# From cross attention to the experts of a decoder layer: three shared groups in source order, with the routing's last steps and the experts' tables between their products

## The chip, the cores and the metric

The kernel runs on one core of a Trainium2 chip. A core has a matrix engine (TensorE, in the profile PE for the products and PEld for its weight loads), three engines for elementwise work (VectorE or DVE, ScalarE or ACT, GpSimd or POOL), and queues that issue transfers: SP for plain loads and stores, ACT for a few, POOL for indirect gathers and scatters. The metric is the device time of one execution in microseconds (us), taken as the median of several runs.

## The reference

A pre-norm decoder layer in float32, for 32 blocks of 128 tokens of 512 features, 4096 tokens in all. Three parts are added to `x` in turn, each on a layer norm of it:

```
x = x + attention(layernorm(x))          # differential self attention, 16 heads, per block
x = x + cross(layernorm(x), ctx)         # cross attention with rotary positions, 8 heads
x = x + ffn(layernorm(x))                # experts and a shared part
```

The last part is what the change touches:

```
scores = sigmoid(x @ gate_w)                       # 32 experts in 4 groups
# the 2 best groups by their best score; of their experts the 6 best
weights = scores of the 6, divided by their sum
expert_out = sum over the 6 of weight * (silu(x @ w_gate[e]) * (x @ w_up[e])) @ w_down[e]
shared = (silu(x @ sw_gate) * (x @ sw_up)) @ sw_down    # 704 wide, every token
return expert_out + shared
```

## The kernel before

The kernel has four stages, which follow each other on TensorE: self attention, cross attention, the experts, and the shared part for those blocks that have not had it earlier.

Cross attention (`CrossAttention`) is software-pipelined by hand. It counts steps, 16 to a block: each step does a piece of one block's scores (`maxima`, `exponentials`, `weigh`), and two lists of due times, `sooner` and `later`, hang other work on the step numbers. `plan` fills them. For block `b`, whose own steps begin at `16 * b`, the outputs leave 16 steps on: `divide` and `turn_out` (a transpose on TensorE each), `leave` (a product, and the store of x2 to `sum_d`), `hand_over` (the normalized h and its transpose are stored to DRAM as `h3_d` and `h3T_d`), `router` (a small product), and then the routing. `run` stops at the last step that has scores. What the last blocks still lack is done by `rest(count)`, which runs `count` more steps of the two lists alone.

The routing (`Routing`) picks for each token six experts. `groups`, `choose` and `take` work on DVE and POOL; `count` puts two small products on TensorE (L934, L935), to know how many tokens came to each expert before; `slots_of` and `enter` write, by an indirect transfer on POOL, each token's number and weight into a table in DRAM, sorted by expert (`table_d`, L951). After the last block `tiles` works out on DVE, in a row of some forty small instructions, which expert each tile of 128 table entries belongs to (`eid`, `fresh`, `rows`).

The shared part (`Shared.group`) works on four blocks at a time. For each of five chunks of 128 of the 704 columns it makes a gate and an up product (L1120, four instructions each of 128x512 outputs, eight records in the profile), a Silu on ACT (L1125) and a multiplication on DVE (L1126, into `s_gu`); the last 64 columns of gate and up share their products (L1134, L1141, L1142). Then, for each of two pairs of blocks, come the products with `sw_down` (L1152, and L1158 for the last chunk), the addition to x2 (`s_x2`, shown as `s_x`, L1162) and the store (L1164). Its inputs are loaded by `load` (`s_hT`, L1103) and at the head of each pair (L1148).

The experts (`Experts`) first gather the table by tiles (L1209), add its two halves (L1216), spread the entries (L1223) and transpose both on TensorE (L1218, L1228); from this come each tile's weights, the rows of DRAM to read (`run_of`, L1251) and to add to. `begin` issues the first tokens' gathers (`tokens`, L1304) and the first four sets of weights (L1278 and on, by SP, which reads the expert's number from `eid`). `run` goes through 208 tiles: `turn_in` (a transpose on DVE, L1316), `gate_up` (L1329), `turn_out` (L1355), `down` (L1365), and a scatter that adds to `sum_d` (L1370).

What orders the work: a scheduler places the instructions on each engine by their priorities and readiness. Inside `tc.manual_schedule(engines=...)` the named engines keep the order of the source. Before the change this holds for `CrossAttention.run` and `Experts.run` (TensorE, DVE, ACT, POOL; SP never), not for the shared groups between them. Each engine runs its own instructions in order.

Tiles come from pools. `cm.banks()` gives one of four PSUM buffers. The pool `s_p` of the shared part is opened when cross attention's pool of exponentials (`xp`) is closed, and lies on its memory; a tile there waits for the last reader of what it covers.

Between cross attention and the experts there are two shared groups (`EARLY = 2`). In the first, `between` is called after each chunk and at the end, and takes from `todo` the routing's last steps:

```
todo = [lambda: cross.rest(16)] * 6 + [
    lambda: routing.tiles(eid, fresh, rows, used, usual),
    lambda: nc.sync.dma_start(out=sum_d[T : T + P, :], in_=rest),
]
```

After it the `Experts` object is built, which includes the tables, then `experts.begin(0, usual)` and the second group. The other six groups come after the experts, with `final=True`, and store to the output.

Of the kernel before, what the change touches and what calls it, by code (L numbers as in the profile page):

```python
# [10 lines left out]
F32 = mybir.dt.float32  # L11
# [446 lines left out]
class CrossAttention:  # L458
# [264 lines left out]
    def plan(self, load_shared):  # L723
# [30 lines left out]
        later.put(20, load_shared)  # L754
        for b in range(self.B):
            sooner.put(2 * S * b - 11, self.measure, b)
# [330 lines left out]
class Shared:  # L1087
# [6 lines left out]
    def __init__(self, cm, pool, w, h3T_d, sum_d, out):  # L1094
        self.cm, self.pool, self.w, self.h3T_d, self.sum_d, self.out = cm, pool, w, h3T_d, sum_d, out
        self.NB = h3T_d.shape[0]
        self.hTs = {}

    def load(self, g):
        G = self.G  # L1100
        if g * G < self.NB and g not in self.hTs:
            self.hTs[g] = self.pool.tile([P, G, EC, P], F32, name="s_hT", bufs=2)
            self.cm.nc.sync.dma_start(  # L1103
                out=self.hTs[g], in_=self.h3T_d[ts(g, G)].rearrange("b p c t -> p b c t")
            )

    def group(self, g, final, between=lambda: None):
# [4 lines left out]
        self.load(g)  # L1112
        self.load(g + 1)
        hT = self.hTs.pop(g)
        gu = pool.tile([P, n + 1, G, P], F32, name="s_gu")
        for m in range(n):
            pgu = cm.banks().rearrange("p two (i t) -> p two i t", i=G)
            for i, part in enumerate((w.gate, w.up)):
                for c in range(EC):
# [3 lines left out]
                    )  # L1123
            act = pool.tile([P, G, P], F32, name="s_act", bufs=2)
# [19 lines left out]
        for pair in range(G // 2):  # L1144
            b = g * G + 2 * pair
            rows = self.sum_d[ts(b // 2, 2 * P), :].rearrange("(b p) e -> p b e", p=P)
            x2 = pool.tile([P, 2, E], F32, name="s_x2", bufs=2)
            nc.sync.dma_start(out=x2, in_=rows)  # L1148
            py = cm.banks()
            for i in range(2):  # L1150
                for m in range(n):
# [3 lines left out]
                    )  # L1155
            for i in range(2):
# [6 lines left out]
            to = self.out[b : b + 2].rearrange("b p e -> p b e") if final else rows  # L1163
            nc.sync.dma_start(out=to, in_=x2)  # L1164
        between()


class Experts:
# [14 lines left out]
    def __init__(  # L1183
# [14 lines left out]
        self.T = T  # L1198

        NT = rows.shape[1]  # L1200
        entry = cm.banks().rearrange("p o (j t) -> p o j t", j=EC)
        parts = cm.banks().rearrange("p o (t j x) -> p (o t) j x", t=2, j=2)
        for j in range(NT):
            got = [
                self.p2.tile([P, E], F32, name="e_y")[:, 0 : 2 * P].rearrange("p (s o) -> p s o", o=2)
                for i in range(len(table_ds))
            ]
            for t, table_d in zip(got, table_ds):
                nc.gpsimd.indirect_dma_start(  # L1209
                    out=t.rearrange("p s o -> p (s o)"),  # L1210
                    out_offset=None,
                    in_=table_d.rearrange("(n s) o -> n (s o)", s=P),
                    in_offset=bass.IndirectOffsetOnAxis(ap=rows[:, j : j + 1], axis=0),
                    bounds_check=table_d.shape[0] // P - 1,
                )
            nc.vector.tensor_tensor(got[0], got[0], got[1], ALU.add)  # L1216
            for o in range(2):
                nc.tensor.transpose(entry[:, o, j, :], got[0][:, :, o], cm.ident)  # L1218

            runs = self.p2.tile([P, self.Q, self.Q, 32], F32, name="e_xr", bufs=3)  # L1220
            slots = got[0][:, :, 0].rearrange("p (b t a) -> p t a b", b=self.Q, t=self.Q)
            for t in range(self.Q):
                nc.vector.tensor_copy(  # L1223
                    runs[:, t].rearrange("p q (a b) -> p q a b", b=self.Q),
                    slots[:, t].unsqueeze(1).broadcast_to([P, self.Q, 32 // self.Q, self.Q]),
                )
            for t in range(self.Q):
                nc.tensor.transpose(  # L1228
                    parts[:, t, j, :], runs[:, t].rearrange("p q i -> p (q i)"), cm.ident
                )  # L1230
        entry = entry.rearrange("p o j t -> p o (j t)")[:, :, 0:n_tiles]
        self.weight = cp.tile([P, n_tiles], F32, name="e_weight")
        nc.vector.tensor_copy(self.weight, entry[:, 1, :])

        row_i = cp.tile([P, 2], I32, name="e_row_i")
        nc.gpsimd.iota(row_i, pattern=[[0, 2]], base=T + 1, channel_multiplier=1)
        nc.vector.tensor_scalar(row_i[:, 1:2], row_i[:, 1:2], -T - 1, None, ALU.add)
        nc.vector.tensor_scalar(row_i[:, 1:2], row_i[:, 1:2], 5, None, ALU.logical_shift_right)
        row = cp.tile([P, 2], F32, name="e_row")
        nc.vector.tensor_copy(row, row_i)  # L1240
        none = cp.tile([P, n_tiles], F32, name="e_none")
        nc.vector.tensor_scalar(none, entry[:, 0, :], 0.0, row[:, 0:1], ALU.is_equal, ALU.mult)
        self.into = cp.tile([P, n_tiles], I32, name="e_into")
        nc.vector.scalar_tensor_tensor(self.into, entry[:, 0, :], -1.0, none, ALU.add, ALU.add)

        self.run_of = cp.tile([P, self.Q, NT * P], I32, name="e_run_of")
        nc.vector.tensor_scalar(
# [131 lines left out]
    def begin(self, first, end):  # L1379

        self.first, self.end, self.last = first, end, None
        for i in range(first, first + 3):
            self.tokens(i)
# [27 lines left out]
def decoder_kernel(  # L1411
# [32 lines left out]
    with tc.tile_pool(name="x_w", bufs=1, side="right") as x_w:  # L1444
# [40 lines left out]
        def between():  # L1485


            if todo:
                todo.pop(0)()
# [81 lines left out]
```

## Time and profile before

| what | value |
|---|---|
| median of 3 runs | 4184.48 us |
| lowest, highest | 4179.18, 4187.29 us |
| the profiled execution's own time | 4186.66 us |
| its span in the profile | 4184.9 us |
| its mean granted TensorE clock | 0.991 |
| TensorE, VectorE, ScalarE, GpSimd busy | 97%, 50%, 31%, 54% of the span |

The profile is of one execution. Its times are counted from the span's start. A line as L1120 is a line of the kernel before. In a timeline, a row gives the start, the length, the engine, the line, the instruction with what it writes and reads, how many follow each other, and in brackets the idle time before it and what ended that. Names are cut of their numbers, so that `s_x2` and `x1` read `s_x` and `x`. The granted clock is the share of full speed that TensorE was given.

Cross attention's last product ends at 2142.07, the experts' first begins at 2296.82, and the first final group's first product begins at 3833.28.

### The profile page before, as it was taken

Reading aid. Unit: us, or ns where it says so; the run is one execution under the profiler, and the core shown is the slowest. Engines: PE = TensorE matmul, PEld = TensorE weight load, DVE = VectorE, ACT = ScalarE, POOL = GpSimd, SP = SyncE. Lnnn points to the kernel's source line nnn. Section 1 sums busy time; section 2 is a strip of 40 time slices with the busy share of each in tenths; the row PEclk is TensorE's granted clock in tenths of the full one; section 3 lists DMA queues with packets and bytes.
Section 4 is the critical chain, followed back from the end, with each engine's and each line's share of the span. In section 5 each row is a group of like instructions: output and inputs, shape, how many; then the busy total and the mean of one; then the engine's idle time right before and its main releaser. Section 6 shows DMA issues by size and latency. Waiting matters only on the chain. (4 is left out here: it accounts for less than half of the span.)

```text
span 4184.9 us, 60374 instructions
## 1 busy us (share of the span) xinstructions
PE 4079.9 (97%) x21044; PEld 2154.4 (51%) x21044; DVE 2093.0 (50%) x3394; ACT 1296.3 (31%) x1855; POOL 2247.7 (54%) x2388
## 2 busy tenths in 40 slices
PE   7999999989999999999989999999999999999999
PEld 5666666653343444443434555555555555554444
DVE  4556555567788888888841333333333333332111
ACT  2333333334565555555630111111111111111000
POOL 3444444343455555555542777777777777773000
PEclk9999999999999999999999999999999999999999
DMA  3000000012111111111114677776776776775110
GB/s 103 26 29 29 29 31 29 16 36 82 41 44 46 44 44 41 44 44 44 36 61 145 164 168 171 165 186 159 169 168 164 168 182 154 185 164 130 60 61 30
DMA packets 282791, 386.33 MB, mean 92 GB/s; under 512 B 147792, under 2 KB 175056, under 8 KB 282448
## 3 DMA queue, kind: packets, MB, share of 16 engines
q0 software_dynamic: 62912, 109.85, 14.6%
q1 hardware_dynamic: 77680, 186.52, 13.6%
q10 hardware_dynamic: 141888, 86.01, 7.4%
q8 instruction: 170, 2.79, 0.3%
q14 instruction: 141, 1.16, 0.1%
HBM read 616.47 MB, written 142.02 MB: 181 GB/s over the span
## 5 line engine op out<-in xcount | busy, mean ns | idle before, releaser
L1304 POOL DMA_INDIRECT e_xr<-h_d,e_run_of x832 | 849.5, 1021 | 296.3 <-issue 246.2
L619 DVE TENSOR_REDUCE nm<-ps 128x2 f32<-128x1024 f32 x512 | 623.7, 1225 | 200.0 <-PE ps L615 131.9
L642 ACT ACTIVATE xp<-ps 128x1024 f32<-128x1024 f32 x512 | 517.1, 1024 | 422.3 <-PE ps L638 421.9
L1334 DVE TENSOR_TENSOR e_gu<-e_act,ps 128x352 f32<-128x352 f32 x208 | 108.6, 522 | 947.8 <-ACT e_act L1333 947.8
L1365 PE MATMUL ps<-wd,e_guT 128*128 128x512 f32 (+1 forms) x1248 | 570.2, 592 | 2.4 <-issue 2.3
L615 PE MATMUL ps<-xk,xq 32*128 32x512 f32 x2048 | 561.4, 635 | 1.6 <-POOL x_ln_down L66 1.1
L638 PE MATMUL ps<-xqn,xk 32*128 32x512 f32 x2048 | 548.8, 639 | 0.6 <-DVE xqn L627 0.6
L1329 PE MATMUL ps<-wg,e_xT 128*128 128x352 f32 x1664 | 529.0, 460 | 4.0 <-DMA wg<-in_L_ffn_w_gate_dram 4.0
L1329 PE MATMUL ps<-wu,e_xT 128*128 128x352 f32 x1664 | 527.2, 460 | 1.6 <-DMA wu<-in_L_ffn_w_up_dram 1.6
L1329 PEld LDWEIGHTS ps<-wg,e_xT 128*128 128x128 f32 x1664 | 315.4, 190 | 239.0 <-issue 105.9
L1329 PEld LDWEIGHTS ps<-wu,e_xT 128*128 128x128 f32 x1664 | 316.1, 190 | 179.7 <-DMA wu<-in_L_ffn_w_up_dram 4.3
L1370 POOL DMA_INDIRECT sum_d<-e_y,e_into x208 | 338.4, 1627 | 118.0 <-issue 70.3
L1333 ACT ACTIVATE e_act<-ps 128x352 f32<-128x352 f32 x208 | 96.4, 463 | 902.6 <-PE ps L1329 797.2
L1365 PEld LDWEIGHTS ps<-wd,e_guT 128*128 128x128 f32 (+1 forms) x1248 | 237.0, 190 | 247.4 <-issue 205.4
L1369 ACT ACTIVATE e_y<-ps,e_weight 128x512 f32<-128x512 f32 x208 | 142.9, 687 | 411.7 <-PE ps L1365 398.0
L615 PEld LDWEIGHTS ps<-xk,xq 32*128 32x128 f32 x2048 | 157.9, 183 | 212.1 <-ACT xp L642 100.7
L951 POOL DMA_INDIRECT table_d<-entry,at x192 | 196.6, 1024 | 109.9 <-DMA table_d<-entry,at 55.7
L1355 DVE STREAM_TRANSPOSE e_guT<-e_gr 96x384 f32<-96x384 f32 (+1 forms) x416 | 230.5, 554 | 47.7 <-DMA e_gr<-e_gu_d 40.4
L653 PE MATMUL ps<-xp,v 128*32 128x512 f32 x2048 | 248.1, 601 | 1.6 <-ACT xp L642 1.2
L1316 DVE STREAM_TRANSPOSE e_xT<-e_xr 128x512 f32<-128x512 f32 x208 | 226.9, 1091 | 6.5 <-DMA e_xr<-h_d,e_run_of 6.5
L229 POOL TENSOR_SCALAR k<-kz,a_keep,a_extra 128x256 f32<-128x256 f32 x128 | 83.4, 660 | 252.3 <-ACT kz L228 246.3
L228 ACT ACTIVATE kz<-ps,a_keep 128x256 f32<-128x256 f32 x128 | 53.7, 470 | 410.9 <-PE ps L222 410.9
(267 smaller groups left out, 5316.8 us busy)
## 6 DMA issues: line engine op xcount, KB each, us to landing
wg<-in_L_ffn_w_gate_dram SPq DMA_DIRECT2D x208, 704.0 KB
wu<-in_L_ffn_w_up_dram SPq DMA_DIRECT2D x208, 704.0 KB
wd<-in_L_ffn_w_down_dram SPq DMA_DIRECT2D x208, 576.0 KB
e_gu_d<-e_gu ACTq DMA_DIRECT2D x208, 192.0 KB
e_gr<-e_gu_d ACTq DMA_DIRECT2D x208, 192.0 KB
wd<-in_L_ffn_w_down_dram SPq DMA_DIRECT2D x208, 128.0 KB
e_xr<-h_d,e_run_of POOLq DMA_INDIRECT x832
xin<-in_x_dram SPq DMA_DIRECT2D x32, 256.0 KB
```

The costliest lines, as they stand in the source:

```text
L615: self.nc.tensor.matmul(sc[:, i, :], q[rows, ts(c, P)], k[rows, :], start=True, stop=True)
L619: self.nc.vector.tensor_reduce(at[:, self.ROW[side], 2 * pair : 2 * pair + 2], sc, AX.X, ALU.max, negate=True)
L638: self.nc.tensor.matmul(sc[:, i, :], k[rows, ts(c, P)], q[rows, :], start=True, stop=True)
L642: self.nc.scalar.activation(e, sc, AF.Exp)
L653: self.nc.tensor.matmul(po[b, side][ts(j, 32), :], self.v2[b % 2][:, c, 2 * j + side, :], es[j // 2][:, j % 2, :], start=c == 0, stop=c == ...
L951: self.nc.gpsimd.indirect_dma_start(out=self.table_ds[k % 2][:, :], out_offset=bass.IndirectOffsetOnAxis(ap=self.at[b][:, k : k + 1], axis=0),
L1304: self.cm.nc.gpsimd.indirect_dma_start(out=xr[:, t, :], out_offset=None, in_=self.h3_d.rearrange("t (q f) -> (t q) f", q=self.Q), in_offse ...
L1316: self.cm.nc.vector.transpose(xT.rearrange("p c (t i) -> p c t i", t=self.Q), self.xr.pop(i).rearrange("p t (j c) -> p c t j", c=EC),)
L1329: nc.tensor.matmul(pgu[:, half, 0:M], t[:, c, :], w[:, c, :], start=c == 0, stop=c == EC - 1)
L1355: self.cm.nc.vector.transpose(t[rows, 0:n, :].rearrange("p c (t i) -> p c t i", t=self.Q), g[rows, :, 0 : 32 * n].rearrange("p t (j c) -> ...
L1365: nc.tensor.matmul(py, t[:n, c, :], self.wd[s][:n, c, :], start=c == 0, stop=c == len(M_CHUNKS) - 1)
L1370: nc.gpsimd.indirect_dma_start(out=self.sum_d[:, :], out_offset=bass.IndirectOffsetOnAxis(ap=self.into[:, i : i + 1], axis=0), in_=y[:, :] ...
```

## The change

The third shared group moves from the end of the kernel to the passage between cross attention and the experts (`EARLY = 3`), so that five groups stay at the end. All three are now under `manual_schedule`, for TensorE, DVE, ACT and POOL.

`between` is called more often in a group: in the middle of each chunk too (after the gate products), and after each block's products within a pair; that is 15 times in a group. The routing's steps come in portions of two (`rest(2)`, 31 times) and spread over the first two groups; what is left of `todo` after them (one portion, `tiles` and one store) follows the second group.

`Experts.__init__` is cut up: `fetch` issues the gathers of the tables, `arrange` adds and spreads them on DVE, `turn_tables` transposes them on TensorE, `places` makes `run_of` and the rest, `first_tokens` gathers the first three tiles' tokens. `experts.begin` (the weights) and `fetch` stand ahead of the third group, the others are called between its products: both `arrange` after the fourth and fifth half chunks, `turn_tables` after the seventh, `places` after the eighth, `first_tokens` after the ninth. Half of the gathered tables are in buffers of `e_xT` instead of `e_y`.

The tiles `s_hT` come from a pool of their own, opened before cross attention's last pools, and the first of them is loaded from `plan`, at step `2 * S * (B - 2)`. The rows of x2 are loaded for a whole group at its head (`load_rows`), and for the third group ahead of `experts.begin`.

```diff
-    def plan(self, load_shared):
+    def plan(self, load_shared, load_tokens):
...
         later.put(20, load_shared)
+        later.put(2 * S * (self.B - 2), load_tokens)
...
     def load(self, g):
         G = self.G
         if g * G < self.NB and g not in self.hTs:
-            self.hTs[g] = self.pool.tile([P, G, EC, P], F32, name="s_hT", bufs=2)
+            self.hTs[g] = self.h_pool.tile([P, G, EC, P], F32, name="s_hT")
...
+    def load_rows(self, g):
+        if g not in self.x2s:
+            self.x2s[g] = []
+            for pair in range(self.G // 2):
+                x2 = self.pool.tile([P, 2, E], F32, name="s_x2", bufs=2)
+                self.cm.nc.sync.dma_start(out=x2, in_=self.rows_of(g, pair))
+                self.x2s[g].append(x2)
...
         self.load(g)
+        self.load_rows(g)
         self.load(g + 1)
...
                         pgu[:, i], part[:, c, ts(m, P)], hT[:, :, c, :],
                         start=c == 0, stop=c == EC - 1,
                     )
+                if i == 0:
+                    between()
...
                         py[:, i, :], gu[:, m, 2 * pair + i, :], w.down[:, m, :],
                         start=m == 0, stop=False,
                     )
+                between()
...
             nc.sync.dma_start(out=to, in_=x2)
-        between()
...
     def begin(self, first, end):
         self.first, self.end, self.last = first, end, None
-        for i in range(first, first + 3):
-            self.tokens(i)
         for i in range(first, first + SETS):
             self.weights_in(i)
             self.weights_out(i)
+
+    def first_tokens(self):
+        for i in range(self.first, self.first + 3):
+            self.tokens(i)
...
-        todo = [lambda: cross.rest(16)] * 6 + [
+        todo = [lambda: cross.rest(2)] * 31 + [
             lambda: routing.tiles(eid, fresh, rows, used, usual),
             lambda: nc.sync.dma_start(out=sum_d[T : T + P, :], in_=rest),
         ]
...
-        EARLY = 2
-        shared.group(0, False, between)
-        while todo:
-            between()
+        EARLY = 3
+        with tc.manual_schedule(engines=in_order):
+            for g in range(EARLY - 1):
+                shared.group(g, False, between)
+            while todo:
+                between()
     e_ctx = ctx.enter_context(ExitStack())
-    experts = Experts(
-        cm, e_ctx, table_ds, h3_d, sum_d, w_gate, w_up, w_down, eid, fresh, rows, n_tiles
-    )
-    experts.begin(0, usual)
-    for g in range(1, EARLY):
-        shared.group(g, False)
+    with tc.manual_schedule(engines=in_order):
+        experts = Experts(
+            cm, e_ctx, table_ds, h3_d, sum_d, w_gate, w_up, w_down, eid, fresh, rows, n_tiles
+        )
+        shared.load_rows(EARLY - 1)
+        experts.begin(0, usual)
+        experts.fetch()
+        nothing = lambda: None
+        todo += [nothing] * 3 + [
+            lambda: experts.arrange(0),
+            lambda: experts.arrange(1),
+            nothing,
+            experts.turn_tables,
+            experts.places,
+            experts.first_tokens,
+        ]
+        shared.group(EARLY - 1, False, between)
+        while todo:
+            between()
     experts.run()
```

`turn_tables` and `places` in the changed kernel, whose lines stood in `Experts.__init__`:

```
    def turn_tables(self):
        nc, cm = self.cm.nc, self.cm
        self.entry_ps = cm.banks().rearrange("p o (j t) -> p o j t", j=EC)
        self.parts_ps = cm.banks().rearrange("p o (t j x) -> p (o t) j x", t=2, j=2)
        for j in range(self.NT):
            got, runs = self.got.pop(j), self.spread.pop(j)
            for o in range(2):
                nc.tensor.transpose(self.entry_ps[:, o, j, :], got[0][:, :, o], cm.ident)
            for t in range(self.Q):
                nc.tensor.transpose(
                    self.parts_ps[:, t, j, :], runs[:, t].rearrange("p q i -> p (q i)"), cm.ident
                )

    def places(self):
        # e_weight, e_row_i, e_row; then run_of (two instructions over 128x1024), none, into
        ...
```

In the built order of the changed kernel, DVE has the two `turn_in` transposes of `Experts.run` directly ahead of the two multiplications of the third group's last chunk (those that stood at L1142).

## The prediction

> **What bounds the kernel now.** I read the page first (busy time, the slices), then the busy time by stretch, then TensorE's waits between cross attention and the experts, then the timelines of all engines there, last the chain that ended last.
>
> ```profile
> PE 4079.9 (97%) x21044; PEld 2154.4 (51%) x21044; DVE 2093.0 (50%) x3394; ACT 1296.3 (31%) x1855; POOL 2247.7 (54%) x2388
> PE   7999999989999999999989999999999999999999
> ```
>
> TensorE is busy 97% of the span and no other engine passes 54%. The change removes no product, so all it can win is time in which TensorE stands idle or runs slowly. Stretch by stretch (length, PE, PEld, DVE, ACT, POOL, granted clock, DMA share, GB/s):
>
> ```profile
> 2142.00:2297.00 155.00, 134.31 (x353) 63.77 (x352) 34.38 (x104) 17.40 (x26) 54.88 (x74) 0.92 0.41 126
> 2297.00:2354.00 57.00, 57.00 (x177) 33.52 (x178) 20.57 (x31) 7.83 (x14) 38.20 (x34) 1.00 0.59 142
> 3892.00:3950.00 58.00, 58.00 (x149) 26.39 (x146) 6.72 (x9) 3.74 (x7) 0.00 (x0) 1.00 0.16 55
> ```
>
> The experts and the final shared groups run without a gap at full clock. The passage between cross attention's last product (2142.07) and the experts' first (2296.82) lacks 21 us of busy time and has a granted clock of 0.92. TensorE's waits there (total, times, longest):
>
> ```profile
> PE ps L934 <- DVE taken L927: 6.1, 2, 3.3
> PE ps L1152 <- DVE s_gu L1126: 5.3, 1, 5.3
> PE ps L1120 <- DMA s_hT<-h3T_d: 4.6, 1, 4.6
> PE ps L1218 <- DVE e_y L1216: 2.4, 1, 2.4
> PE ps L83 <- DVE xo L674: 1.3, 1, 1.3
> ```
>
> And what follows a wait, in TensorE's timeline (start, length, in brackets the idle time before):
>
> ```profile
> 2146.68 5.82 PE L1120 MATMUL ps<-s_hT,sg 128*128 128x512 f32 x8 [4.60 <-DMA s_hT<-h3T_d]
> 2152.33 3.60 PE L1120 MATMUL ps<-s_hT,su 128*128 128x512 f32 x8
> ...
> 2174.30 5.38 PE L1120 MATMUL ps<-s_hT,sg 128*128 128x512 f32 x8
> ...
> 2187.29 6.00 PE L1120 MATMUL ps<-s_hT,sg 128*128 128x512 f32 x8
> ...
> 2215.73 7.11 PE L1152 MATMUL ps<-sd,s_gu 128*128 128x512 f32 x12 [5.26 <-DVE s_gu L1126]
> ```
>
> Eight such records take 3.60 us at full clock; after a wait they take 5.4 to 6.0.
>
> **What the passage holds at least.** One shared group without gaps is read from the chain that ended last (start, length):
>
> ```profile
> 3949.95 34.53 PE ps L1120 x80
> ...
> 4007.42 34.53 PE ps L1120 x80
> ```
>
> 57.47 us from start to start. The routing's last steps put on TensorE (timeline 2155.77 to 2187): rows of 1.04, 0.63, 1.12, 0.60, 0.31, 0.39, 1.08, then 0.60, 0.41, 0.39, 1.06, then 0.41 and 0.39 at full clock, 8.4 us; each of eleven rows overlaps the next by 0.09, so 7.4. The experts' table transposes: six take 0.77 (2233.68 to 2234.45), twelve 1.5. With two groups: 114.9 + 7.4 + 1.5 = 123.8. The passage takes 154.75, so 30.9 us are excess. Idle are 4.60 + 1.33 + 0.68 + 0.31 + 2.80 + 3.33 + 5.26 + 2.38 = 20.7; the other 10.2 are slow products: 2.2, 1.8 and 2.4 in the three L1120 rows shown, 1.9 in the L1152 row (twelve at 0.437 would be 5.25), some 2 around the tables.
>
> **The change part by part.**
>
> *A third group early.* It leaves the tail and enters the passage: 57.47 against 57.47, nothing. The experts' start of before, in like terms, is 2296.82 + 57.47 = 2354.29.
>
> *The s_hT wait.* Its tiles get a pool of their own and no longer lie on cross attention's xp tiles. On SP both loads now stand far ahead, among the loads of cross attention; before, they were issued at 2140.50, behind the store of h. So the first gate product follows at 2142.07. The 4.60 and the 2.2 after it go: the clock in 2140 to 2142 is 1.00 and falls to 0.54 only in 2144 to 2146, in the idle time. What is late next is leave's xoT (below).
>
> *The steps between.* `rest(16)` six times becomes `rest(2)` 31 times, two calls per chunk, so that some 3.44 us of products stand between steps whose chains were back to back. With the rows of before: xo (0.36 + 0.76 on DVE after the xu transposes) has 3.44 us, no wait; xoT sits on ACT behind a table load (1.28) and a Silu (0.60), some 2.7 us after the `up` products, and has 4.0, no wait; the first `taken` starts after the second chunk's multiplication on DVE (17.9 us into the group), takes 2.7 (2140.86 to 2143.52) and is asked for at 20.5: 0.3 us. The two later counts have more room, one five products of the pairs (4.3 us), one a whole half chunk. I take 1 us for all of them; bounds 0 and 8.4 (what these waits cost before, 1.33 + 0.68 + 0.31 + 2.80 + 3.33).
>
> *Source order on DVE and the tables.* Let X be the end of the second group. DVE first adds its last pair (1.3), then runs all of `tiles`: 18 instructions that stood far earlier before, and 21 that depend on `next`, each about 0.19: rows at X+7.6, fresh at X+8.7. POOL's six `enter` transfers stand behind the second group's steps, not its last product, and are through by then. The four gathers at 1.3 each: X+7.9 to X+12.9. Before, a gather's data came 6.5 us after its issue ended with the DMA share at 1.02 (2207.25 to 2213.78), and 3.6 at 0.84 (2235.47 to 2239.10); I take 6.5: X+19.4. Both `arrange` (1.3 each): X+20.8. The transposes stand after seven half chunks: X+24.0. No wait, 3 us to spare; the 2.4 and the 5.3 (DVE held the multiplication behind L1216) go.
>
> *What is late next.* `places` follows the fourth chunk's multiplication (X+30.7): run_of at X+33.5. POOL issues the tokens from X+33.7, 1.31 each: the second tile's fourth ends at X+43.9. Landing: 4.6 us after the first tile's last issue in before (2248.54 to 2253.16), 1.7 after the second's (2253.79 to 2255.46). In the changed order both `turn_in` transposes (1.10 each) stand on DVE ahead of the two multiplications of the last chunk (L1142's), which the end product of the first pair (L1158's) needs. Those two are then done at X+48.0; TensorE asks at X+39.5 + 8.6 = X+48.1. This is a tie, so each us of lateness is a us of stall. I take 2 us, bounds 0 and 6.4 (tokens 4 us late, plus 2.4 of slow products).
>
> [...] After waits of 2.80 and 3.33 us the next eight products took 5.38 and 6.00, not 3.60. [...] I price by the rows: my 2 us are a stall of 1, and 1 for the chance of slow products after it.
>
> *At nothing, and under what cover.* The ACT table loads (five before, five in the new order) lie beside products; PSUM has four buffers, two of which cover a late Silu; uncovered, 1.28 each. The x2 loads go out at a group's start and wait on SP for the last group's stores; needed 48 us later. [...] x_p2 and x_pT move up 16 KB: the first xp is written at 968.64, the last xres under it leaves SP at 964.11; two us late would be two us. The copy of 12 blocks to the output instead of 8: before, it and the first loads of s_x took 3842 to 3854; with half as much again some 18 us, and s_x is wanted 38 us after the issue. Weights: first issue X+10, first use X+59.
>
> **Sum.** 2142.07 + 3 x 57.47 + 7.4 + 1.5 = 2323.4; with 1 and 2: 2326.4. Against 2354.29: 27.9 us less. The profiled execution has a span of 4184.9 (4186.66 outside), the median of the three runs is 4184.48; so 4157.0 as a span and 4156.6 as a median: 4157.
>
> **The rivals.**
>
> *The tables come late.* Weights (8.65 MB from X+10 on) and gathers share the DMA engines. If the gathers land 10 us later, TensorE waits 7 at the transposes, with 2.4 of slow products after it, and what follows moves with it: 27.9 - 9.4 leaves 18.5, so 4166. For: share 1.02 in 2200 to 2210. Against: 3.6 and 6.5 us under that very load. 0.19.
>
> *The waits return elsewhere.* Thirty places of about 1 us would eat everything: 4184. For: order on TensorE is fixed, any late step stops all products. Against: 3.44 us at each place where 2.7 is the longest chain. 0.04.
>
> *Slower.* DVE stands in `arrange` until the gathers land; behind it are the multiplications that free PSUM, and TensorE stands at the transposes. If the gathers came only after all four weight sets, at the 170 GB/s of the experts' stage (8.65 MB, 51 us): X+61, a stall of 61 + 2 - 24 = 39, and 2.4: 13 us worse than before, 4198. It is slower from a landing at about X+58 on, 45 us after the last issue. Against: the same 3.6 and 6.5. 0.03.
>
> That the change doesn't do what it says is excluded by the new instruction order, which has the three groups and the steps where the source has them.
>
> **How the numbers follow.** First case 0.74, tables late 0.19: faster 0.93. Same 0.04, slower 0.03; 0.2% is 8.4 us, about the spread of the three runs, and what a measurement of this kernel can tell from no change. Low end: all 30.9 us, and 4 of spread: 4149. High end: tables late (18.5) less half the upper bound of the waits between (4.2), 14 us gained: 4171.
>
> **What would show it.** Right: PE's waits between the last L653 and the first expert product sum to under 6 us, with none on s_hT and none at L1218's transposes; the granted clock of that passage over 0.98; the experts' start near 2326; five final groups at 57.47. Wrong: a wait of the table transposes on DVE, or one of over 5 us at the first pair's end product of the third group, or a last L653 product that ends at another time than 2142.

## The result, and the profile after

The changed kernel takes 4154.94 us (median, 4152.99 to 4156.72), the kernel before 4182.24 in the runs beside it (4179.18 to 4187.29): a ratio of 0.9925, with a 95% interval of 0.9914 to 0.9935. The forecast was 4157. In the later runs, from e4 on, every kernel took about 50 us longer, the one before too (its medians there are 4234.94 to 4247.53), nearly all of it in the experts' stage (1581 to 1598 us); so a run is compared only by its ratio to the kernel before, measured beside it.

The profiled execution has a span of 4151.3 (4152.99 outside it) and a granted clock of 0.995. Its times below count from the start of its own span; "passage" is, here and in all that follows, the time from the end of cross attention's last product (L653) to the start of the experts' first. The two engine lines first, busy time and slices:

```profile
PE 4063.8 (98%) x21044; PEld 2148.4 (52%) x21044; DVE 2092.0 (50%) x3394; ACT 1295.9 (31%) x1855; POOL 2248.9 (54%) x2388
...
PE   7999999989999999999999999999999999999999
```

The same 21044 matmul records take 16 us less, about 9 of them in the passage with the third group counted in: most of its slow products are gone, and with them the dip of the old slices. What moved is best seen in the busy time of the passage (length, PE, PEld, DVE, ACT, POOL, granted clock, DMA share, GB/s):

```profile
2140.00:2324.00 184.00, 182.77 (x498) 86.71 (x494) 43.98 (x136) 21.15 (x33) 55.59 (x76) 0.99 0.36 112
```

and in TensorE's waits over that stretch (total, times, longest):

```profile
PE ps L1178 <- DVE s_gu L1163: 1.2, 1, 1.2
PE ps L653 <- ACT xp L642: 1.0, 1, 1.0
```

The second belongs to cross attention and stood there before too (1.2). So of 20.7 us of waits one is left, at the place that the prediction had named. Its neighbourhood in the timeline of PE and DVE (start, length, in brackets the idle time before and what ended it):

```profile
2300.98 8.75 PE L1171 MATMUL ps<-sd,s_gu 128*128 128x512 f32 x20
...
2309.36 1.09 DVE L1358 STREAM_TRANSPOSE e_xT<-e_xr 128x512 f32<-128x512 f32 x1 [2.30 <-DMA e_xr<-h_d,e_run_of]
...
2310.47 0.42 DVE L1163 TENSOR_TENSOR s_gu<-s_act,ps 64x256 f32<-64x256 f32 x1
...
2310.95 1.98 PE L1178 MATMUL ps<-sd,s_gu 64*128 64x512 f32 x4 [1.23 <-DVE s_gu L1163]
2311.35 0.41 DVE L1163 TENSOR_TENSOR s_gu<-s_act,ps 64x256 f32<-64x256 f32 x1 [0.45 <-ACT s_act L1162]
...
2312.86 10.55 PE L1171 MATMUL ps<-sd,s_gu 128*128 128x512 f32 x20
...
2324.40 2.63 PE L1371 MATMUL ps<-wg,e_xT 128*128 128x352 f32 x8
```

DVE stands in front of the second `turn_in` until its tokens land (2.30), and the multiplication that TensorE needs is behind it in the order: its Silu had ended at 2301.56 and the products it reads at 2301.14, but it began at 2310.47. TensorE is idle for 1.23, then waits inside the L1178 row for the second multiplication (1.98 instead of 1.13), and then twenty products take 10.55 instead of 8.85. The stall costs 1.23 + 0.85 + 1.70 = 3.8 us.

The final groups in the chain that ended last (start, length) are what they were, 57.46 from start to start:

```profile
3973.43 34.53 PE ps L1139 x80
...
4030.89 34.53 PE ps L1139 x80
```

Where the 33.6 us between the two spans (4184.9 and 4151.3) lie: the passage went from 154.75 with two groups, 212.2 if the third group's 57.47 is added, to 183.6: 28.6 us. Cross attention's last product ended 1.3 earlier. The experts, from their first product to the first final group's, took 1534.1 instead of 1536.5: 2.4. The tail, with the third group taken out, took 1.3 less. The last three, 5 us, are chance between executions as far as these runs tell. In the second profile of the changed kernel (e0) the same three differ from this one by 0.4, 4.3 and 1.7 us, and the two medians lie only 27.3 apart, less than the passage alone. Part of the 5 us is the clock: the profile of before has stretches at half of it in the experts' stage, after a wait of 4.02 for weights, and at the first final group, after a wait of 1.81, and this one has none there (1.00 from 2320 to 4140; before, the columns as above):

```profile
2984.00:2990.00 6.00, 5.23 (x9) 3.16 (x10) 0.00 (x0) 0.00 (x0) 4.78 (x5) 0.50 0.92 227
3834.00:3837.00 3.00, 3.00 (x4) 1.14 (x4) 0.00 (x0) 0.00 (x0) 1.04 (x1) 0.50 0.23 43
```

They don't go with one of the kernels: in e0, the changed kernel too, the first 80 products of the first final group take 36.27 us, where those of the other four take 34.53.

### The profile page after: what moved, and what is told of

Same layout as the page of the kernel before. It is cut to its first block, busy times and chain, and to the rows that moved or that the text cites. A ratio compares the mean times of both kernels' runs of the same rounds, so it can differ in the third digit from the quotient of the medians.

```text
span 4151.3 us, 60361 instructions
## 1 busy us (share of the span) xinstructions
PE 4063.8 (98%) x21044; PEld 2148.4 (52%) x21044; DVE 2092.0 (50%) x3394; ACT 1295.9 (31%) x1855; POOL 2248.9 (54%) x2388
## 5 line engine op out<-in xcount | busy, mean ns | idle before, releaser
L1407 PE MATMUL ps<-wd,e_guT 128*128 128x512 f32 (+1 forms) x1248 | 569.9, 592 | 2.1 <-issue 2.0
L1407 PEld LDWEIGHTS ps<-wd,e_guT 128*128 128x128 f32 (+1 forms) x1248 | 237.3, 190 | 246.3 <-issue 202.9
L653 PE MATMUL ps<-xp,v 128*32 128x512 f32 x2048 | 247.7, 600 | 1.4 <-ACT xp L642 1.0
```

What stands on the lines that cost most here:

```text
L653: self.nc.tensor.matmul(po[b, side][ts(j, 32), :], self.v2[b % 2][:, c, 2 * j + side, :], es[j // 2][:, j % 2, :], start=c == 0, stop=c == ...
L1407: nc.tensor.matmul(py, t[:n, c, :], self.wd[s][:n, c, :], start=c == 0, stop=c == len(M_CHUNKS) - 1)
```

## The experiments

Times are compared as ratios to the kernel before in the same batch of runs, and mechanisms by the passage of the profiled run. The passages, with 57.47 us added where only two groups are in it:

| run | what | passage, three groups | ratio to before, 95% interval |
|---|---|---|---|
| (before) | | 212.2 | |
| (after) | | 183.6 | 0.9925 [0.9914, 0.9935] |
| e0, e9 | the changed kernel again | 180.2, 183.6 | 0.9928 [0.9915, 0.9942], 0.9926 [0.9907, 0.9945] |
| e1, e10 | `turn_in` later on DVE | 179.8, 179.8 | 0.9922 [0.9909, 0.9936], 0.9927 [0.991, 0.9944] |
| e2 | `s_hT` as before | 187.1 | 0.9938 [0.9925, 0.9952] |
| e3 | routing's steps in coarse portions | 200.9 | 0.9974 [0.9967, 0.998] |
| e4 | tables ahead of the third group | 201.3 | 0.9976 [0.9966, 0.9985] |
| e5 | two groups, portions of five | 198.5 | 0.9975 [0.9966, 0.9984] |
| e6 | before, with three groups | 215.0 | 1.0 [0.9991, 1.0009] |
| e7 | before, with `s_hT`'s own pool | 207.4 | 0.9987 [0.9979, 0.9995] |
| e8 | two groups, portions by hand | 188.7 | 0.9953 [0.9937, 0.9969] |
| e11 | e8 with `turn_in` later | 183.6 | 0.9931 [0.9913, 0.9949] |

**e0: the changed kernel again.** No edit; it ran beside e1, e2 and e3.

> The changed kernel once more, on the chip and beside the variants of it that follow. My theory: TensorE's waits in the passage between cross attention and the experts are what the change takes away, so the ratio to the kernel before is near 0.9934 (27 us of 4182), and TensorE's waits from 2140 to the experts' first product are again about 1.2 us, all at the end product of the third group's first pair. Rival: part of the gain seen first (5 us of the 33 between the two profiled spans lie outside the passage) belongs to the change; then the ratio is 0.9920 or less.

4156.04 us (4152.13 to 4159.44). The ratio's interval, 0.9915 to 0.9942, holds 0.9934 and 0.9920 alike, so the time doesn't tell the theory from its rival. In its profiled run the tie on DVE fell the other way: no idle time stands before L1178, only 0.45 us of waiting inside it (1.58 instead of 1.13), and the passage was 180.2:

```profile
2310.09 1.58 PE L1178 MATMUL ps<-sd,s_gu 64*128 64x512 f32 x4
```

The tokens of the first and the second tile landed 3.5 and 1.6 us after the last issue of each had ended, against 5.2 and 3.3 in the run above; the source is the same, so the difference of 3.4 us between the two passages goes with this landing.

**e1: the tie broken in the source.** The two `turn_in` transposes leave the head of `Experts.run` and stand behind the last chunk's multiplications on DVE:

```diff
+    def first_turns(self):
+        for i in range(self.first, self.first + 2):
+            self.turn_in(i)
+            self.tokens(i + 3)
...
-            for i in range(first, first + 2):
-                self.turn_in(i)
-                self.tokens(i + 3)
...
             experts.first_tokens,
+            nothing,
+            experts.first_turns,
...
         experts.first_tokens()
+        experts.first_turns()
         experts.run()
```

> The changed kernel with the first two turn_in (and the tokens' gathers behind them) called between the third group's products, after the multiplications of its last chunk, instead of at the head of Experts.run. My theory: the one wait left (1.23 us, for the multiplications that stood behind the second turn_in on DVE, with 0.85 + 1.70 us of slow products after it) goes: 3.8 us less than the changed kernel, ratio 0.9925, no wait in the passage, and its granted clock at 1.00. Rival: a wait moves to the experts' first product, since turn_in is now later by the two multiplications (1.7 us): then the time stays within 1 us of the changed kernel.

4152.66 us (4148.55 to 4156.22), 3.4 under e0 by medians. DVE and PE in its timeline:

```profile
2301.17 0.42 DVE L1163 TENSOR_TENSOR s_gu<-s_act,ps 64x256 f32<-64x256 f32 x1 [2.54 <-ACT s_act L1162]
2302.04 0.41 DVE L1163 TENSOR_TENSOR s_gu<-s_act,ps 64x256 f32<-64x256 f32 x1 [0.45 <-ACT s_act L1162]
2304.27 1.10 DVE L1358 STREAM_TRANSPOSE e_xT<-e_xr 128x512 f32<-128x512 f32 x1 [1.81 <-DMA e_xr<-h_d,e_run_of]
...
2309.24 1.13 PE L1178 MATMUL ps<-sd,s_gu 64*128 64x512 f32 x4
```

The multiplications are now done 7 us before TensorE asks for them, and the tokens are still in time: the experts' first product doesn't wait. In the old order a late landing stalls TensorE, in this one it did not. The passage of 179.8 is the shortest that any run showed; three groups without a gap are 172.4 of it. The medians do not show the gain by themselves, since the intervals of e0 and e1 overlap.

**e2: `s_hT` back on cross attention's memory.** Its pool and its early load are undone:

```diff
-            self.hTs[g] = self.h_pool.tile([P, G, EC, P], F32, name="s_hT")
+            self.hTs[g] = self.h_pool.tile([P, G, EC, P], F32, name="s_hT", bufs=2)
...
-        later.put(2 * S * (self.B - 2), load_tokens)
...
-        s_h_pool = ctx.enter_context(tc.tile_pool(name="s_h", bufs=2, reuse_waits="tile"))
-        shared = Shared(cm, s_h_pool, h3T_d, sum_d, out)
...
+        shared = Shared(cm, s_pool, h3T_d, sum_d, out)
```

> The changed kernel with the tiles s_hT back in the pool of the shared part, on the memory of the exponentials, and without the early load. My theory: the first gate product waits again for the load: 4.6 us of idle time and 2.2 of slow products, 6.8 us more than the changed kernel (ratio about 0.995); the rest of the passage as it was. Rival one: the wait came from SP's order (the loads behind the store of h), and a scheduler that places the load elsewhere hides it: no difference. [...]

The passage grew from e0's 180.2 to 187.1. The wait is back, and the slow eight behind it (the waits, then the timeline of PE):

```profile
PE ps L1138 <- DMA s_hT<-h3T_d: 4.4, 1, 4.4
```
```profile
2144.55 5.75 PE L1138 MATMUL ps<-s_hT,sg 128*128 128x512 f32 x8 [4.36 <-DMA s_hT<-h3T_d]
```

4.4 and 2.1 (5.75 instead of 3.60): the 6.8 of the prediction within 0.3. The medians differ by 3.1 only (4159.18 and 4156.04), half of what the passage shows, and the intervals of the two ratios overlap: by time alone e2 isn't shown to be slower.

**e3: the routing's steps in four portions of sixteen.**

```diff
-        todo = [lambda: cross.rest(2)] * 31 + [
+        todo = [lambda: cross.rest(16)] * 4 + [lambda: None] * 27 + [
```

> The changed kernel with the routing's last steps in four portions of 16 at the first four places, nothing at the next 27, and tiles where it was. My theory: the waits of the kernel before come back, since the steps' chains stand back to back again: 8.4 us idle (1.33, 0.68, 0.31, 2.80, 3.33) and 4 to 7 us of slow products after 2.80 and 3.33: 12 to 15 us more than the changed kernel, ratio about 0.997. [...] Rival: order on DVE fixed by the source makes the counts wait for whole chunks' multiplications, over 20 us more.

4174.9 us, 18.9 over e0; the passage is 20.7 over e0's. TensorE's waits in it:

```profile
PE ps L935 <- DVE taken L928: 7.5, 3, 3.5
PE ps L83 <- ACT h L74: 2.7, 1, 2.7
PE ps L83 <- DVE xo L674: 1.3, 1, 1.3
...
PE ps L691 <- ACT xoT L682: 0.7, 1, 0.7
```

12.2 us of waits, and 8.5 of slower products behind them, so the lengths of the waits alone do not price it. The direction held; the size was underestimated (12 to 15), because three counts wait, where two did before, and h comes late once. For the first count the reason can be seen on DVE. Its `taken` was written long ahead of it in the kernel before, where the scheduler had put the block's `choose` and `take` earlier; in source order they stand behind the addition of the portion's own x (before, then e3):

```profile
2143.05 0.47 DVE L927 TENSOR_REDUCE taken<-hits 128x32 f32<-128x192 f32 x1
```
```profile
2151.39 0.47 DVE L928 TENSOR_REDUCE taken<-hits 128x32 f32<-128x192 f32 x1
```

The count began at 2160.84 before, without a wait, and at 2152.01 in e3, after a wait of 2.05. But e3 also sets its portions a half chunk apart, 3.44 us, where the kernel before had a whole chunk between them. How much of the 20.7 us comes from the larger portions, the source order or the smaller distance was not separated.

**e4: the tables ahead of the third group.** `fetch`, `arrange`, `turn_tables`, `places` and `first_tokens` all run before the third group, and `manual_schedule` around them is left out:

```diff
-        nothing = lambda: None
-        todo += [nothing] * 3 + [
-            lambda: experts.arrange(0),
...
-        shared.group(EARLY - 1, False, between)
+    experts.arrange(0)
+    experts.arrange(1)
+    experts.turn_tables()
+    experts.places()
+    experts.first_tokens()
+    shared.group(EARLY - 1, False)
```

> The changed kernel with all of the experts' tables ahead of the third group, and that group left to the scheduler; the first two groups unchanged. In the built order the twelve table transposes stand on TensorE directly after the second group. My theory: without the seven half chunks as cover TensorE waits for what was hidden: the second arrange ends 21 to 22 us after the second group (in the profile of the changed kernel at 2283.85, 22.1 after 2261.75), so about 21 us idle and 2 of slow products, less the 3.8 of the wait that then has no place: 19 to 20 us more than the changed kernel, ratio about 0.998. Rival: the gain comes from the first group's steps and the load, the tables were never the point: within 6 us of the changed kernel.

The passage is 201.3, 21.1 over e0's. TensorE stands at the transposes:

```profile
PE ps L1275 <- DVE e_y L1258: 14.7, 1, 14.7
PE ps L1275 <- DVE e_xT L1258: 4.5, 1, 4.5
```

19.2 of waits, where about 21 were expected, and about 2 of slow products. Against the execution that lost the tie (183.6) it is 17.7 more, where 19 to 20 were expected. This is the full length of the chain rows, gathers, landing, addition, when nothing covers it; the kernel before showed only 2.4 + 5.3 of it, since its chain ran beside the first group's products (`fresh` was written at 2192.59, 41 us ahead of the first transposes).

**e5: two early groups, portions of five.** The question was what the third group is for: cover of its own for the tables, or only more room.

```diff
-        todo = [lambda: cross.rest(2)] * 31 + [
+        todo = [lambda: cross.rest(5)] * 13 + [
...
-        EARLY = 3
+        EARLY = 2
```

> The changed kernel with EARLY = 2: the routing's last steps in portions of five over the first group, the tables between the second group's products. My theory: the third group has no worth of its own; the steps in portions of five bring back the waits of xo and xoT (2.0 us) and little else, so 2 to 5 us more than the changed kernel, ratio 0.994 to 0.9946. Rival: two groups are too short a cover, the tables come late, and 10 us or more are lost.

The passage is 141.0, or 198.5 with a third group added: 18.3 over e0's. My 2 to 5 us were wrong. The rival's size was right and its cause was not: the table transposes do not wait. The waits are those of e3:

```profile
PE ps L935 <- DVE taken L928: 7.1, 3, 4.0
PE ps L83 <- DVE xo L674: 1.3, 1, 1.3
PE ps L83 <- ACT h L74: 1.2, 1, 1.2
...
PE ps L691 <- ACT xoT L682: 0.7, 1, 0.7
```

Five steps in a portion put `choose`, `take` and `count` of some blocks into one call, so that the count's products stand directly behind a chain on DVE and POOL that has just begun. Whether the third group matters was left open by this run; e8 and e11 take it up.

**e6: the kernel before, with three groups in the passage** (`EARLY = 3`, nothing else).

> The kernel before with EARLY = 3 alone. My theory: a group moves from the end to the passage, no wait is covered by it since the table transposes stay behind the first group: 0, ratio 0.999 to 1.001. Rival: the scheduler finds room for tables and tokens beside one group more: 5 to 12 us less than before, ratio 0.997 to 0.999.

Ratio 1.0 [0.9991, 1.0009], passage 215.0 against 212.2, with the old waits (the one on `s_gu` at 6.7 instead of 5.3). Moving a group by itself gains nothing, as expected.

**e7: the kernel before, with `s_hT` in its own pool and loaded early.** The diff is the change's own for `plan`, `load` and the pool.

> The kernel before with the pool of its own for s_hT and the early load alone. My theory: the wait of 4.6 us and the 2.2 of slow products after it go, the others stay: 6.8 less, ratio 0.9984. Rival: the products come 6.8 us earlier, the routing's chains do not, and what is won is waited for at the next step (the first xo, or the counts, or the gathers): 0 to 3 less.

Ratio 0.9987 [0.9979, 0.9995], 5.5 us by it; the passage is 149.9, 4.8 less than before, not 6.8. The wait on `s_hT` is gone, but the later one at the second pair's products is 6.8 instead of 5.3. That it grew because the first one is gone isn't shown: in e6, which still has the wait on `s_hT` (4.2), it is as long (e6, then e7):

```profile
2215.06 8.16 PE L1152 MATMUL ps<-sd,s_gu 128*128 128x512 f32 x12 [6.74 <-DVE s_gu L1126]
```
```profile
2210.67 8.27 PE L1156 MATMUL ps<-sd,s_gu 128*128 128x512 f32 x12 [6.79 <-DVE s_gu L1130]
```

Against e6, from the same batch, e7's passage is 7.6 shorter (207.4 and 215.0), so the 6.8 lies between the two comparisons. The tables came earlier too: DVE began to write `fresh` 50.5 us after cross attention's last product before, and 43.4 in e7.

**e8: two groups, portions cut by hand,** so that a block's `take` is at least half a chunk ahead of its `count`.

```diff
-        todo = [lambda: cross.rest(2)] * 31 + [
+        nothing = lambda: None
+        todo = [
+            (lambda n=n: cross.rest(n)) if n else nothing
+            for n in (2, 2, 4, 2, 6, 0, 8, 2, 6, 8, 3, 19, 0)
+        ] + [nothing] * 2 + [
...
-        EARLY = 3
+        EARLY = 2
```

> Two shared groups early instead of three, six at the end, as in e5, but the routing's steps cut by hand into portions of 2, 2, 4, 2, 6, 0, 8, 2, 6, 8, 3 and 19, so that each block's choose and take stand at least a half chunk ahead of its count and nothing else of a block is asked for in the portion that makes it. If the third group is worth nothing but room for such portions: the passage (last L653 product to the experts' first) is 57.47 us shorter than that of the changed kernel, 180.2 - 57.5 = 122.7, plus waits of 0 to 3 us, and the time is that of the changed kernel to within 3 us (ratio to before 0.992 to 0.9935). If the third group itself carries the tables: they are asked for 24 us after the end of the first group, with the last enters on POOL only a few us before, so TensorE stands at the table transposes for 5 us or more, and the time is 5 to 10 us over the changed kernel (ratio 0.994 to 0.9955).

Neither expectation holds as written. The passage is 131.25, or 188.7, 8.5 over e0's. Both this and the ratio 0.9953 are what the second expectation gives, but its cause is wrong, since the waits are not at the tables:

```profile
PE ps L935 <- DVE taken L928: 2.2, 1, 2.2
PE ps L1178 <- DVE s_gu L1163: 2.2, 1, 2.2
```

One count still stands too close behind its `take`, and the tie of the changed kernel is lost by 2.2 here, with 4.2 of slow or waiting products after it.

**e9: the changed kernel beside e8.**

> The changed kernel itself, unchanged, on the chip of the two beside it. Ratio to before 0.9925 within 0.0015; the wait of the third group's first end product (L1178) is 0 to 2 us, as the order of the gathers' landing falls out.

Ratio 0.9926 [0.9907, 0.9945], passage 183.6 with the wait of 1.23 at L1178, the same as in the first profile to a hundredth.

**e10: e1 beside e8 and e9.**

> As e1: the two turn_in transposes on DVE behind the last chunk's multiplications, nothing else changed. If the tie on DVE costs what the profile of the changed kernel shows when it is lost (1.2 us of wait and 1.7 of slow products, in part of the executions), the median is 0 to 3 us under that of the changed kernel beside it. If the 3.4 us of e1 were chance between runs, the two medians agree within 1 us.

No wait, passage 179.8 as in e1. The medians are 1.4 apart (4206.33 and 4207.73), and the intervals overlap almost wholly. In the profiles, the changed kernel loses the tie in two of three executions, and its passage is then 3.8 us longer than e1's; e1's order never does in two. By time alone the version of e1 is the fastest that was run, but not shown to be faster than the changed kernel.

**e11: e8 with the order of e1.**

> e8 with the edit of e10: the two turn_in transposes on DVE behind the last chunk's multiplications. If e8's wait of 2.17 us at its second group's first end product (L1178), and the 4.2 us of slow products after it, come from the order on DVE, they go: the passage is 131.25 - 6.4 = 124.9 us, and with one shared group of 57.47 added 182.3, 2.1 over that of the changed kernel without a wait (180.2); what is left is the count's wait of 2.2. If they come from late tokens because the first group alone leaves POOL's transfers too late, the wait moves to the experts' first product, and the passage stays at 130 or more.

The L1178 wait is gone; one is left in the passage:

```profile
PE ps L935 <- DVE taken L928: 1.8, 1, 1.8
```

The passage is 126.2 (183.6 with a third group), between the expected 124.9 and the rival's 130; the 1.3 more are slow products behind this wait. So two groups are worth what the changed kernel's three are, apart from one count that is 2 us short of room, which costs 3.5 with its slow products; ratio 0.9931 [0.9913, 0.9949] against 0.9927 [0.991, 0.9944] of e10. The third group is not needed for the tables. What it gives is places: 31 portions of two steps instead of portions chosen by hand. Whether still better portions would make two groups equal to three wasn't tried.

## Why the prediction was right

The forecast was 4157 against a measured 4154.94, and 27.9 us in the passage against 28.6. The signs named for it came: 1.2 us of waits in the passage, none on `s_hT` and none at the table transposes, a granted clock of 0.99 there and the experts' start at 2324.40. One sign of being wrong came too, a last L653 product at 2140.79 and not at 2142. As far as these runs tell, that is no effect of the change: e6, which is as the kernel before up to there, has it at 2139.95, and e8, which is as the changed kernel up to there, at 2143.02.

*A third group costs in the passage what it saves in the tail.* e6: ratio 1.0.

*The minimum.* The prediction had 3 x 57.47 + 7.4 + 1.5 = 181.3. The passage without any wait is 179.8: the routing's products and the table transposes together take 7.4, not 8.9. The sum had taken 0.09 for the overlap of a routing row with the next; in both profiles it is about 0.17 where no wait lies between. The table transposes take 1.34, not 1.5.

*The `s_hT` wait,* 4.6 and 2.2: e2 brings back 4.4 and 2.1. Nothing took its place.

*The steps between:* 1 us taken, none measured. The shortest cover, the first count with its forecast of 0.3, held. e3 shows what that room is worth: 20.7.

*The tables.* With X the end of the second group (2261.75): `rows` was written at X+6.9 (forecast X+7.6), `fresh` at X+8.2 (8.7), the last gather's issue ended at X+12.8 (12.9). Then POOL's last gather and DVE's second addition:

```profile
2273.55 1.01 POOL L1244 DMA_INDIRECT e_xT<-table_d,rows  x1 [0.30 <-issue]
```
```profile
2282.53 0.43 DVE L1258 TENSOR_TENSOR e_xT<-e_xT 128x256 f32<-128x256 f32 x1 [4.20 <-DMA e_xT<-table_d,rows]
```

The data came 8.0 us after the issue ended, not 6.5, so both `arrange` were done at X+22.1 (forecast X+20.8). The transposes came at X+24.1, and 2 of the 3 us of spare time were left. The rival "tables late" would have begun to cost time from a landing another 2 us later. (By its own terms, the rival "slower" would begin at a landing of X+47.5, where a stall of 25.5 and 2.4 of slow products eat the 27.9; the X+58 that stands there doesn't follow.)

*The tie on DVE.* Forecast were multiplications done at X+48.0 and asked for at X+48.1, with 1 us of stall and 1 of slow products taken. TensorE asked at X+48.0; the multiplications were done at X+49.1 and X+50.0. Place and cause were right. Mis-sized was the landing of the second tile's tokens: 3.3 us after their last issue, where the sum had 1.7 from before. Mis-sized too was what a short stall brings with it: 1 taken for slow products, and 1.70 of them came, with 0.85 more inside the stalled row. The bounds of 0 and 6.4 hold the 3.8, and both sides of the tie were seen, 0.45 in e0 and 3.8 in e9.

*The sum of these.* Against the forecast the minimum gave 1.5 more, the waits between 1.0 more, and the tie 1.8 less: 0.7 in all. That it came so close is in part luck, for the three errors are each larger than what is left of them. The median missed by 2.1 because the forecast started from 4184.48, and the kernel before took 4182.24 in the runs beside the changed one, 2.2 less.

*The slow products behind the tie.* By its length alone the stall would cost 1.2. The granted clock by single us after the wait of 1.23 (the granted clock is the third figure from the end):

```profile
2312.00:2313.00 1.00, 1.00 (x4) 0.24 (x3) 0.03 (x1) 0.00 (x0) 0.70 (x2) 1.00 0.25 66
2313.00:2314.00 1.00, 1.00 (x2) 0.50 (x3) 1.00 (x1) 0.00 (x0) 0.94 (x1) 0.65 0.27 66
2314.00:2315.00 1.00, 1.00 (x2) 0.34 (x1) 0.19 (x1) 0.00 (x0) 0.76 (x1) 0.50 0.26 66
```

It fell to 0.50, for 3.4 us (2313.3 to 2316.7), and the twenty products behind the stall took 1.7 us more (10.55 instead of 8.85). Pricing by the rows was right in kind.

*The gain is not the sum of its parts.* Undone one by one, the edits cost 6.9, 20.7 and 21.1 (e2, e3, e4), 48.7 together, where the whole brings 32. Source order is a reason that can be argued for: it can make a coarse portion or a late table dearer than the scheduler's own order had made them before, as the first count of e3 shows. But e3 also has a smaller distance between its portions than the kernel before, and the tables of e4 begin only behind the steps, which the fine portions spread over two groups. Source order as such, the early loads of x2 and the split of the tables over two buffers were not undone by themselves.

## What to carry to other kernels

When an engine's order is fixed by the source, ask for every small product that is woven in how long its producers' chain is, and put at least that much independent work between the portion that starts the chain and the one that uses it; a portion that holds both costs the chain (in e5 three counts waited 7.1 us). Look for what stands in front of a producer on its own engine: here two transposes that wait for gathers stood ahead of two multiplications that were wanted sooner, and exchanging them removed the last stall from the profiles. And before a longer wait downstream is put down to a wait removed upstream, look for it in a run where nothing was removed: the 6.8 of e7 stood in e6 as well.

## What the runs showed of the hardware

A short wait cost more than itself in several places, by products that ran slowly behind it. In the changed kernel the granted clock was 0.50 for 3.4 us after the wait of 1.23 at L1178. In the passage of the kernel before it was 0.50 five times, once at each of these waits:

| wait, us | from, to | clock at 0.50 from | for, us |
|---|---|---|---|
| 4.60 (L1120) | 2142.08, 2146.68 | 2144.2 | 6.8 |
| 2.80 (L934) | 2170.14, 2172.94 | 2174.9 | 3.4 |
| 3.33 (L934) | 2183.11, 2186.44 | 2185.1 | 6.8 |
| 5.26 (L1152) | 2210.47, 2215.73 | 2215.9 | 3.4 |
| 2.38 (L1218) | 2237.19, 2239.57 | 2239.8 | 3.4 |

It fell 2.1 us into the wait of 4.60 and 2.0 into that of 3.33, but only 2.0 us after the end of that of 2.80, 2.4 after that of 1.23, and 0.1 to 0.2 after the ends of the other two. The five starts lie 30.7, 10.2, 30.7 and 23.9 us apart, which is 9, 3, 9 and 7 times the shorter stretch of 3.41. The waits of 1.33 in the kernel before (L83) and of 2.01 and 1.70 in the changed one (L1407, L1139, from 3851.9 to 3858.5) left the clock at 1.00.

In the other runs the rows tell the same. Behind a wait of 1.82 (e11) fifteen products took 8.38 instead of 6.60; behind 3.52 (e3), 3.96 and 2.26 (e5) eight took 5.38, 6.29 and 6.48 instead of 3.60; behind 2.17 (e8) twenty took 11.21 instead of 8.85. The longer waits slowed what followed too: behind the 14.7 and 4.5 of e4 the rows of the table transposes took 0.67 to 1.06 instead of 0.39 to 0.60, and behind the 6.7 of e6 twelve products took 8.16, where those behind the 5.26 of the kernel before took 7.11. But behind the 2.74 of e8, at cross attention's end, eight took 3.70, and behind the 1.18 of e5 six took 2.74, as they do without a wait. So the length of a wait alone does not decide it in these runs; what does wasn't settled.

An indirect gather's landing varied more than its issue here. In both executions of the changed kernel that are shown the four table gathers were issued 1.3 to 1.4 us apart; the last one's data came 8.0 and 7.6 us after its issue had ended, where the kernel before showed 6.5 and 3.6. The token gathers of the first two tiles landed 5.2 and 3.3 us after their last issue in one execution of the changed kernel, and 3.5 and 1.6 in another (e0). That moved the multiplications behind them in DVE's order, and with them the stall of TensorE, from 3.8 us to 0.45.
